# The front of a fused scan-and-experts kernel in another order, with list factors for eight columns at once

## The chip, the cores and the metric

The kernel runs on one core of one Trainium2 chip. The metric is the device time of one execution in microseconds (us), as the median of several runs. A profiled execution is shown beside it: its span runs from the first to the last recorded instruction, and its own time is a little longer than its span.

## The reference

For x of shape (2, 2048, 256) the layer norm xn (without weights) feeds two branches, and the result is x + scan branch + expert branch.

```python
x = L0_attn_x
xn = _layernorm(x, axis=-1)
x = x + _L0_attn_ref(xn, ...) + _L0_ffn_ref(xn, ...)

# scan branch: sort the tokens of each batch by nearest mean, scan, put them back
buckets = argmax(l2norm(xn) @ l2norm(means).T)          # 8 means
sort_idx = argsort(buckets, stable=True); xs = xn[sort_idx]
x_dbl = x_proj_weight @ xs                              # dts (32), B (16), C (16)
C += (means @ prompt_weight.T)[buckets of the sorted tokens]
delta = softplus(dt_projs_weight @ dts + bias); A = -exp(A_logs)
h = exp(delta*A)*h + delta*u*B; y = sum(h*C) + D*u      # 256 channels x 16 states
out = y in the old order of the tokens

# expert branch: 8 experts, the best two of each token
logits = xn @ w_gate; top 2; probs = softmax over the two
y_e = (silu(xn @ w1_e) * (xn @ w3_e)) @ w2_e            # hidden 512
out = sum over the two of probs * y_e
```

Both branches need an order of tokens that is known only at run time: the scan needs the tokens sorted by bucket, the experts need them in tiles of 128 that belong to one expert.

## The kernel before

**Front.** `normalize(b, xts)` is called once per batch (two batches of 2048 tokens, J = 16 columns of 128). It takes the statistics (L337 to L348), 1/sqrt by `rsqrt` (L244 to L253: a square root on ScalarE, L247, then a reciprocal and one Newton step on VectorE), normalises 16 columns in place (L358), writes them to the DRAM tensor `xn_d` (L362), transposes them (L370, L371) and multiplies with the normalised means and the gate weights (L374). After a second transpose, `sc` holds the bucket scores (L394) and `lg_all` the gate logits (L399).

`sort_tokens` (L404 to L456) finds each token's bucket and its position in the sorted order. `list_rows(b, pos)` (L458) turns positions into a list: which token stands at each position. `route` (L463) finds the two best experts, a slot for each of the 2 x 4096 choices, the expert of each of the NT = 71 tiles and hence the rows of the weights to load (`w_row`, L526), the list of tokens by slot (`token_of`, L510), and each token's share of the two experts, written beside the tokens into `xn_d` (L539).

`list_tokens` (L298 to L329) makes such a list with TensorE. For each column of 128 tokens a one-hot matrix of the place's low 7 bits (`one`, L315) is multiplied (L321) with a one-hot row of the high bits, scaled with two parts of the token's number (`num`, L317). The products of all columns add up in PSUM. The scan's list has 16 columns for one batch, the experts' list 64 columns. Both factors are built column by column on VectorE.

**Order of the front.** The text calls `normalize` for both batches, `sort_tokens`, `list_rows(0, pos)`, the gather of the first piece (L549), `route`, then the gathers of the first tiles' tokens (`load_rows`, L778) and weights (`load_up`, `load_down`, L764), then everything of the first scan piece up to its step sizes (`turn` L570, `project` L584, `end_projection` L589 to L592, `load_b` L609, `load_z` L597, `step_size` L621 to L627, `square` L631, `series` L642 to L651, `mask_z` L605). This part of the text is put on the engines by a scheduler that may move an instruction ahead of others on its own engine when it expects its inputs earlier. A pool of small tiles (`front`) is closed after `route`; the third set of weight buffers lies in the memory that it frees.

**The main stage** is in the order of the text on each engine (chained by the last lines of the kernel). Eight scan pieces (2 batches, 4 pieces of 512 tokens) give 64 steps of four places each; a place is one `feed` (L695), one `scan` (L704) on VectorE and one `decay` (L689) on ScalarE, with the turning (L716, L720) and contraction (L725) of the step before. Between the places the text deals out 213 expert jobs (71 tiles: two of `up`, L804, and one of `down`, L827), so that TensorE's and VectorE's planned work keep a fixed ratio. The first `ahead` = 5 jobs stand before the first scan place:

```python
ahead = 5
for n in range(ahead):
    jobs[n]()
    ...
pieces[0].begin(0)
pieces[0].begin(1)
for i in range(Q):
    steps[0].decay(i)
steps[0].feed(0)
```

`at_place(2, 3, lambda: list_rows(1, pos), 2.5, 7.0)` puts the second batch's list into the third step. When the last job is given, `acc_d` (which starts as a copy of x, L240, and takes the expert rows and the scan's rows) is copied to the output (L1026); the last piece is added there (L745).

Of the kernel before, what the change touches and what calls it, by code (L numbers as in the profile page):

```python
# [60 lines left out]
def scan_moe_kernel(  # L61
# [55 lines left out]
    slot = [cst.tile([P, BJ], I32, name=f"slot{k}") for k in range(2)]  # L117
# [14 lines left out]
    def load_x(b: int, j0: int, pool=tok):  # L132
# [18 lines left out]
    idx_l = cst.tile([P, BJ, K], F32, name="idx_l")  # L151
# [5 lines left out]
    idx_m = cst.tile([P, BK, J], F32, name="idx_m")  # L157
# [4 lines left out]
    keep = cst.tile([P, BK, J], F32, name="keep")  # L162
    nc.vector.memset(keep, 1.0)
    nc.vector.memset(keep[:, :, 0:1], 0.0)
    keep2 = cst.tile([P, E, BJ], F32, name="keep2")
# [8 lines left out]
    idx_p = cst.tile([P, 2, P], BF16, name="idx_p")  # L174
    nc.gpsimd.iota(
        idx_p, pattern=[[0, 2], [1, P]], base=0, channel_multiplier=0,
# [3 lines left out]
    token = cst.tile([P, BJ], I32, name="token")  # L180
    nc.gpsimd.iota(
        token.rearrange("p (b j) -> p b j", b=B), pattern=[[L, B], [1, J]], base=1,
        channel_multiplier=J,
    )
    parts = cst.tile([P, BJ, 2], F32, name="parts")
    for i, (op, by) in enumerate(((ALU.logical_shift_right, 6), (ALU.bitwise_and, 63))):
        part = cst.tile([P, BJ], I32, name=f"part{i}")
        nc.vector.tensor_scalar(part, token, by, None, op)
        nc.vector.tensor_copy(parts[:, :, i], part)
# [50 lines left out]
    nc.sync.dma_start(acc_d[0 : B * L, :], x.rearrange("b l d -> (b l) d"))  # L240
# [3 lines left out]
    def rsqrt(r, v, shape):  # L244

        s = sml.tile(shape, F32, tag="rs_s", name="rs_s")
        nc.scalar.activation(s, v, AF.Sqrt)  # L247
        nc.vector.reciprocal(r, s)
        t = sml.tile(shape, F32, tag="rs_t", name="rs_t")
        nc.vector.tensor_mul(t, v, r)  # L250
        nc.vector.tensor_mul(t, t, r)
        nc.vector.tensor_scalar(t, t, -0.5, 1.5, ALU.mult, ALU.add)
        nc.vector.tensor_mul(r, r, t)  # L253
# [29 lines left out]
    def over(v, last_dim):  # L283
        return v.unsqueeze(2).to_broadcast([P, v.shape[1], last_dim])

    def first_of_max(v, tag):

        n = v.shape[1]
        m = sml.tile([P, n], F32, tag=f"m{tag}", name="fm_m")
        nc.vector.tensor_reduce(m, v, AX.X, ALU.max)  # L290
        c = sml.tile([P, n, K], F32, tag="fm_c", name="fm_c")
        nc.vector.tensor_tensor(c, v, over(m, K), ALU.is_equal)
        nc.vector.tensor_mul(c, c, idx_l[:, 0:n, :])
        i = sml.tile([P, n], F32, tag=f"i{tag}", name="fm_i")
        nc.vector.tensor_reduce(i, c, AX.X, ALU.min)
        return m, i

    def list_tokens(places, parts, width: int, tag: str):  # L298


        pl = ps_m.tile([P, 2, width], F32, tag="m", name="pl")
        cols = []
        for k, place in enumerate(places):
            n = place.shape[1]
            fs = []
            for what, op, by in (("lo", ALU.bitwise_and, P - 1), ("hi", ALU.logical_shift_right, 7)):
                v = lst.tile([P, n], I32, tag=f"{tag}i", name="v", bufs=1)
                nc.vector.tensor_scalar(v, place, by, None, op)
                f = lst.tile([P, n], F32, tag=f"{tag}{what}{k}", name="f", bufs=1)
                nc.vector.tensor_copy(f, v)  # L310
                fs.append(f)
            cols += [(fs, i) for i in range(n)]
        for m, ((lo, hi), i) in enumerate(cols):
            one = lst.tile([P, P], BF16, tag="one", name="one")
            nc.vector.tensor_scalar(one, idx_p[:, 0, :], lo[:, i : i + 1], None, ALU.is_equal)  # L315
            num = lst.tile([P, 2, width], BF16, tag=f"num{tag}", name="num")
            nc.vector.scalar_tensor_tensor(  # L317
                num, idx_p[:, :, 0:width], hi[:, i : i + 1],
                parts[:, i, :].unsqueeze(2).to_broadcast([P, 2, width]), ALU.is_equal, ALU.mult,
            )  # L320
            nc.tensor.matmul(  # L321
                pl.rearrange("p a q -> p (a q)"), lhsT=one, rhs=num.rearrange("p a q -> p (a q)"),
                start=m == 0, stop=m == len(cols) - 1,
            )
        hi = lst.tile([P, width], F32, tag=f"{tag}h", name="hi", bufs=1)
        nc.vector.tensor_scalar_mul(hi, pl[:, 0, :], 64.0)
        tokens = lst.tile([P, width], F32, tag=f"{tag}t", name="tokens", bufs=1)
        nc.vector.tensor_add(tokens, hi, pl[:, 1, :])
        return tokens  # L329

    sc = cst.tile([P, BJ, K], F32, name="sc")

    def normalize(b: int, xts):
# [16 lines left out]
        rsqrt(rstd, ve, [P, J])  # L350


        psc = ps_h.tile([P, CH], F32, tag="h0", name="psc")
        for j0 in range(0, J, JC):
            xn = xts[j0 // JC]
            for i in range(JC):
                j = j0 + i
                nc.vector.tensor_scalar(  # L358
                    xn[:, i, 0:D], xn[:, i, 0:D], nm[:, j : j + 1], rstd[:, j : j + 1],
                    ALU.add, ALU.mult,  # L360
                )
# [42 lines left out]
    def sort_tokens():  # L404

        _, bk = first_of_max(sc, "b")
        oh = sml.tile([P, BK, J], F32, tag="oh1", name="oh")
# [50 lines left out]
    def list_rows(b: int, pos):  # L458
        own = slice(b * J, (b + 1) * J)
        tokens = list_tokens([pos[:, own]], parts[:, own, :], J, "s")  # L460
        nc.vector.tensor_scalar(line_of[b], tokens, -1.0, None, ALU.add)

    def route():  # L463
# [3 lines left out]
        m1, i1 = first_of_max(lg, "1")  # L467
        oh1 = sml.tile([P, BJ, E], F32, tag="oh1", name="oh1")
        nc.vector.tensor_tensor(oh1, idx_l, over(i1, E), ALU.is_equal)
        nc.vector.scalar_tensor_tensor(lg, oh1, LOWEST, lg, ALU.mult, ALU.add)  # L470
        m2, i2 = first_of_max(lg, "2")
        oh2 = sml.tile([P, BJ, E], F32, tag="oh2", name="oh2")
        nc.vector.tensor_tensor(oh2, idx_l, over(i2, E), ALU.is_equal)

        both = sml.tile([P, E, BJ], F32, tag="at", name="both")
        nc.vector.tensor_add(both.rearrange("p e j -> p j e"), oh1, oh2)
# [24 lines left out]
        for oh, s in ((oh1, slot[0]), (oh2, slot[1])):  # L501
            at = sml.tile([P, BJ, E], F32, tag="at", name="at_slot")
            nc.vector.tensor_mul(at, oh, cum.rearrange("p e j -> p j e"))
            sf = sml.tile([P, BJ], F32, tag="sf", name="sf")
            nc.vector.tensor_reduce(sf, at, AX.X, ALU.add)
            nc.vector.tensor_copy(s, sf)
        tokens = list_tokens(slot, parts, NT, "e")
        none = sml.tile([P, NT], F32, tag="none", name="none")
        nc.vector.tensor_scalar(none, tokens, 0.0, spare, ALU.is_equal, ALU.mult)
        nc.vector.scalar_tensor_tensor(token_of, tokens, -1.0, none, ALU.add, ALU.add)  # L510

# [26 lines left out]
        for b in range(B):  # L538
# [3 lines left out]
            )  # L542

# [293 lines left out]
    pos = sort_tokens()  # L837
    pieces = [Piece(b, c) for b in range(B) for c in range(NCH)]
    tiles = [Tile(t) for t in range(NT)]
    list_rows(0, pos)  # L840
    pieces[0].gather()
    route()
# [4 lines left out]
    for t in tiles[:NW]:  # L847
        t.load_rows()
        t.load_up()
    for t in tiles[:NW]:  # L850
        t.load_down()
# [68 lines left out]
    ahead = 5  # L920
# [159 lines left out]
```

## Time and profile before

| | us |
|---|---|
| median of 3 runs (lowest, highest) | 829.47 (824.61, 829.79) |
| the profiled execution's own time | 832.5 |
| its span | 830.7 |
| VectorE (DVE) busy | 740.2 |
| TensorE (PE) busy | 723.6 |
| GpSimd (POOL) busy | 526.3 |
| ScalarE (ACT) busy | 492.6 |

In the profile, PEld is TensorE's load of the stationary operand, SPq the queue that issues the plain DMAs, POOLq the one that issues the indirect ones, and L317 is line 317 of the kernel. Busy time is the time in which at least one instruction of the engine is recorded as running; one of TensorE's matmuls has a modelled end, so a busy TensorE is not one at its peak. A granted clock of 1.0 (PEclk) is the full TensorE clock. The duration of an instruction is longer than the distance between two starts where consecutive instructions overlap.

### The profile page before, as it was taken

How to read it: one execution, taken by the hardware profiler on the slowest of the kernel's cores; microseconds unless marked ns; L12 is line 12 of the kernel's file. 1: busy time of each engine (PE TensorE's matmuls, PEld its weight loads, DVE VectorE, ACT ScalarE, POOL GpSimd, SP SyncE). 2: the span in 40 equal slices, each digit the busy share in tenths (PEclk: the TensorE clock that was granted, in tenths of full speed). 3: DMA queues.
4: the chain of work that ended last, by engine and by line, in shares of the span. 5: the costliest groups of instructions: out<-in, count | busy, mean ns of one | idle time of the engine just before them, and what ended most of it. 6: DMA issues, size and time to landing. Idle time of an engine off the chain costs nothing.

```text
span 830.7 us, 17111 instructions
## 1 busy us (share of the span) xinstructions
PE 723.6 (87%) x6548; PEld 601.4 (72%) x6548; DVE 740.2 (89%) x1363; ACT 492.6 (59%) x957; POOL 526.3 (63%) x373
## 2 busy tenths in 40 slices
PE   0953759999999999999999998999899989999963
PEld 0322239678987889788878986799779977899842
DVE  7659888889988999999999995899889996999992
ACT  2420225476567767686668563866677666857662
POOL 1004047657777678788878886687767677677413
PEclk9975559999999999999999998999999999999996
DMA  9804732357446754684568366647754765334562
GB/s 298 295 37 47 289 99 61 79 144 250 120 116 165 230 142 114 157 255 122 134 159 257 75 185 145 177 103 206 209 130 102 245 188 112 93 59 125 97 203 39
DMA packets 61185, 125.92 MB, mean 152 GB/s; under 512 B 24488, under 2 KB 42064, under 8 KB 53808
## 3 DMA queue, kind: packets, MB, share of 16 engines
q0 software_dynamic: 40224, 65.03, 34.5%
q1 hardware_dynamic: 20880, 59.80, 20.8%
q8 instruction: 52, 0.85, 0.4%
q14 instruction: 29, 0.24, 0.1%
HBM read 180.06 MB, written 27.00 MB: 249 GB/s over the span
## 4 chain that ended last, share of the span: by engine, by line
PE 55%; DVE 8%; ACT 7%; DMA 6%; issue 4%; POOL 2%; POOLq 0%; SPq 0%; ACTq 0%; DVEq 0%
PE p_ps L804 23%; PE py L827 12%; PE pt_s L716 9%; PE y L725 5%; DMA xs<-xn,line_of 3%; DVE hs L704 3%; ACT ht L720 2%; DVE bu L695 2%; DMA out_dram<-acc 2%; PE px L584 1%; ACT da L689 1%; PE pt_g L787 1%; DMA acc<-yo,token_of 1%; PE pt_u L570 1%; PE px L589 1%
## 5 line engine op out<-in xcount | busy, mean ns | idle before, releaser
L804 PE MATMUL p_ps<-xT,w 128*128 128x128 f32 x2272 | 281.9, 280 | 0.8 <-ACT xT L789 0.5
L804 PEld LDWEIGHTS p_ps<-xT,w 128*128 128x128 f32 x2272 | 269.5, 195 | 15.5 <-issue 7.6
L704 DVE TENSOR_TENSOR_SCAN hs<-da,carry,bu 128x512 f32<-128x512 f32 x192 | 246.4, 1284 | 0.0
L689 ACT ACTIVATE da<-dl,na 128x512 f32<-128x512 f32 x256 | 183.1, 726 | 1.1 <-DVE hs L704 1.0
L745 POOL DMA_INDIRECT acc<-yo,token_of x71 | 143.4, 2020 | 54.9 <-ACT yo L831 18.3
L695 DVE TENSOR_TENSOR bu<-du,bt 128x512 f32<-128x512 f32 x256 | 173.9, 680 | 0.0
L720 ACT COPY ht<-pt_s 128x512 f32<-128x512 f32 x256 | 137.5, 593 | 22.8 <-PE pt_s L716 21.3
L716 PE MATMUL pt_s<-ident,hs 128*128 128x128 f32 x1024 | 136.9, 277 | 14.8 <-ACT ht L720 7.9
L827 PE MATMUL py<-w,g 128*128 128x256 f32 x568 | 135.6, 382 | 5.6 <-ACT u L571 2.3
L716 PEld LDWEIGHTS pt_s<-ident,hs 128*128 128x128 f32 x1024 | 116.4, 142 | 31.5 <-ACT ht L720 13.8
L778 POOL DMA_INDIRECT xg_sb<-xn,token_of x71 | 93.2, 1313 | 53.3 <-DVE token_of L510 32.0
L764 POOL DMA_INDIRECT w<-in_w_up_dram,w_row x71 | 91.1, 1284 | 52.7 <-PE p_ps L804 17.4
L827 PEld LDWEIGHTS py<-w,g 128*128 128x128 f32 x568 | 102.3, 190 | 19.4 <-ACT u L571 3.3
L764 POOL DMA_INDIRECT w<-in_w_down_dram,w_row x71 | 94.6, 1333 | 21.6 <-issue 14.0
L549 POOL DMA_INDIRECT xs<-xn,line_of x32 | 43.0, 1344 | 72.1 <-DVE fm_m L532 62.6
L812 ACT ACTIVATE t_sb<-p_ps 128x512 f32<-128x512 f32 x71 | 42.7, 601 | 65.1 <-PE p_ps L804 61.6
L704 DVE TENSOR_TENSOR_SCAN hs<-da,bu 128x512 f32<-128x512 f32 x64 | 78.3, 1223 | 1.1 <-ACT da L689 1.1
L831 ACT ACTIVATE yo<-py,own 128x256 f32<-128x256 f32 x71 | 34.1, 481 | 71.8 <-PE py L827 58.7
L725 PE MATMUL y<-ht,z 128*32 128x128 f32 x2048 | 75.2, 284 | 1.3 <-ACT ht L720 0.8
L817 DVE SCALAR_TENSOR_TENSOR t_sb<-t_sb,p_ps 128x512 f32<-128x512 f32 x71 | 48.3, 681 | 24.0 <-ACT t_sb L812 21.1
L725 PEld LDWEIGHTS y<-ht,z 128*32 128x32 f32 x2048 | 52.8, 112 | 23.0 <-issue 13.2
L745 POOL DMA_INDIRECT acc<-yt,line_of x28 | 50.9, 1818 | 21.6 <-issue 9.6
(198 smaller groups left out, 690.8 us busy)
## 6 DMA issues: line engine op xcount, KB each, us to landing
bt<-bc SPq DMA_DIRECT2D x32, 1024.0 KB
z<-bc SPq DMA_DIRECT2D x32, 256.0 KB
xn<-xt SPq DMA_DIRECT2D x8, 520.0 KB
xt<-in_x_dram SPq DMA_DIRECT2D x8, 512.0 KB
w<-in_w_up_dram,w_row POOLq DMA_INDIRECT x71
w<-in_w_down_dram,w_row POOLq DMA_INDIRECT x71
xg_sb<-xn,token_of POOLq DMA_INDIRECT x71
acc<-yo,token_of POOLq DMA_INDIRECT x71
```

What stands on the lines that cost most here:

```text
L689: nc.scalar.activation(self.da[i], self.piece.dl[:, self.h, :], AF.Exp, scale=na[:, self.h, n : n + 1])
L695: nc.vector.tensor_mul(self.bu[i], self.piece.du[:, self.h, :], self.piece.bts[self.q][:, i, :])
L704: nc.vector.tensor_tensor_scan(self.hs[:, :, i], self.da[i], self.bu[i], start, ALU.mult, ALU.add)
L716: nc.tensor.transpose(pt[:, j, :], self.hs[:, t0 : t0 + G, :].rearrange("p t n -> p (t n)"), ident)
L720: nc.scalar.copy(self.ht[i], pt)
L725: nc.tensor.matmul(p.ys[self.h][j * G : (j + 1) * G, i, :], lhsT=p.zs[q][:, i * (P // G) + j, :], rhs=self.ht[i][:, j, :], start=False, st ...
L745: ins = nc.gpsimd.indirect_dma_start(out=to, out_offset=bass.IndirectOffsetOnAxis(ap=numbers, axis=0), in_=rows, in_offset=None, compute_o ...
L764: nc.gpsimd.indirect_dma_start(out=to[self.t % NW], out_offset=None, in_=rows, in_offset=bass.IndirectOffsetOnAxis(ap=w_row[:, self.t : se ...
L778: nc.gpsimd.indirect_dma_start(out=self.xg, out_offset=None, in_=xn_d, in_offset=bass.IndirectOffsetOnAxis(ap=token_of[:, self.t : self.t ...
L804: nc.tensor.matmul(p[:, f, :], lhsT=wk[:, h, f * P : (f + 1) * P], rhs=self.xT[:, h, :], start=h == 0, stop=h == ND - 1,)
L817: nc.vector.scalar_tensor_tensor(self.s, self.s, 1.0, self.p1, ALU.add, ALU.mult)
L827: nc.tensor.matmul(py, lhsT=self.g[:, f, :], rhs=w2[:, f, :], start=f == 0, stop=f == NH - 1)
```

## The change

- **Order.** After `normalize` the text calls `route`, gathers the first three tiles' tokens and the first two tiles' weights, and only then calls `sort_tokens` and `list_rows(0, pos)` and gathers the first piece. The third set of weights is loaded after that, when the front's pool is closed. Inside `route` the list of the experts comes last, behind the weights' rows and the shares. Best-expert and bucket searches (`first_of_max`) run per batch. `ahead` is 14.
- **List factors.** `list_tokens` builds `one`, and the one-hot part of `num`, for LC = 8 columns in one VectorE instruction each, in bfloat16 with the column innermost; the two scaled parts of `num` are one ScalarE and one VectorE instruction for eight columns. The token's number is now 16 x partition + column instead of 64 x high part + low part. TensorE still makes one matmul per column, reading both factors with a step of eight elements.
- **1/sqrt.** `rsqrt` starts from an integer guess on the bits and makes three Newton steps, all on VectorE.
- **Smaller edits.** The last of each four columns is normalised on ScalarE; the copy of x into `acc_d` is issued after the writes of `xn_d`; some constants move to the front's pool.

```diff
-    idx_p = cst.tile([P, 2, P], BF16, name="idx_p")
+    LC = 8
+    idx_p = cst.tile([P, P, LC], BF16, name="idx_p")
...
-    nc.sync.dma_start(acc_d[0 : B * L, :], x.rearrange("b l d -> (b l) d"))
...
     def rsqrt(r, v, shape):
 
-        s = sml.tile(shape, F32, tag="rs_s", name="rs_s")
-        nc.scalar.activation(s, v, AF.Sqrt)
-        nc.vector.reciprocal(r, s)
+        guess = sml.tile(shape, I32, tag="rs_g", name="rs_g")
+        nc.vector.tensor_scalar(guess, v[:].bitcast(I32), 1, None, ALU.logical_shift_right)
+        nc.vector.tensor_scalar(
+            r[:].bitcast(I32), guess, -1.0, float(0x5F3759DF), ALU.mult, ALU.add
+        )
         t = sml.tile(shape, F32, tag="rs_t", name="rs_t")
-        nc.vector.tensor_mul(t, v, r)
-        nc.vector.tensor_mul(t, t, r)
-        nc.vector.tensor_scalar(t, t, -0.5, 1.5, ALU.mult, ALU.add)
-        nc.vector.tensor_mul(r, r, t)
+        for _ in range(3):
+            nc.vector.scalar_tensor_tensor(t, v, -0.5, r, ALU.mult, ALU.mult)
+            nc.vector.tensor_mul(t, t, r)
+            nc.vector.scalar_tensor_tensor(r, t, 1.5, r, ALU.add, ALU.mult)
...
-        for m, ((lo, hi), i) in enumerate(cols):
-            one = lst.tile([P, P], BF16, tag="one", name="one")
-            nc.vector.tensor_scalar(one, idx_p[:, 0, :], lo[:, i : i + 1], None, ALU.is_equal)
-            num = lst.tile([P, 2, width], BF16, tag=f"num{tag}", name="num")
-            nc.vector.scalar_tensor_tensor(
-                num, idx_p[:, :, 0:width], hi[:, i : i + 1],
-                parts[:, i, :].unsqueeze(2).to_broadcast([P, 2, width]), ALU.is_equal, ALU.mult,
-            )
-            nc.tensor.matmul(
-                pl.rearrange("p a q -> p (a q)"), lhsT=one, rhs=num.rearrange("p a q -> p (a q)"),
-                start=m == 0, stop=m == len(cols) - 1,
-            )
+        for m in range(n // LC):
+            own = slice(m * LC, (m + 1) * LC)
+            one, num = factors(width)
+            nc.vector.tensor_tensor(
+                one, idx_p, lo[:, own].unsqueeze(1).to_broadcast([P, P, LC]), ALU.is_equal
+            )
+            nc.vector.tensor_tensor(
+                num[:, 2], idx_p[:, 0:width, :], hi[:, own].unsqueeze(1).to_broadcast([P, width, LC]),
+                ALU.is_equal,
+            )
+            b = of_batch[m]
+            j0 = m * LC % J
+            nc.scalar.activation(num[:, 0], num[:, 2], AF.Copy, scale=part_p[:, b : b + 1])
+            nc.vector.tensor_mul(
+                num[:, 1], num[:, 2],
+                part_j[:, j0 : j0 + LC].unsqueeze(1).to_broadcast([P, width, LC]),
+            )
+            for i in range(LC):
+                nc.tensor.matmul(
+                    pl, lhsT=one[:, :, i], rhs=num[:, 0:2, :, i],
+                    start=m == 0 and i == 0, stop=m == n // LC - 1 and i == LC - 1,
+                )
...
     for b in range(B):
         normalize(b, xts[b * NCH : (b + 1) * NCH])
-    pos = sort_tokens()
+    nc.sync.dma_start(acc_d[0 : B * L, :], x.rearrange("b l d -> (b l) d"))
     pieces = [Piece(b, c) for b in range(B) for c in range(NCH)]
     tiles = [Tile(t) for t in range(NT)]
+    route()
+    for t in tiles[:NW]:
+        t.load_rows()
+    for t in tiles[: NW - 1]:
+        t.load_up()
+        t.load_down()
+    pos = sort_tokens()
     list_rows(0, pos)
     pieces[0].gather()
-    route()
     front.close()
     late = ctx.enter_context(tc.tile_pool(name="late", bufs=1))
     w13_sb.append(late.tile([P, 2 * ND * H], F32, name=f"w13_{NW - 1}"))
     w2_sb.append(late.tile([P, NH * D], F32, name=f"w2_{NW - 1}"))
-    for t in tiles[:NW]:
-        t.load_rows()
-        t.load_up()
-    for t in tiles[:NW]:
-        t.load_down()
+    tiles[NW - 1].load_up()
+    tiles[NW - 1].load_down()
...
-    ahead = 5
+    ahead = 14
```

The new factor tiles of the front lie in the buffers that held x (`front_factors`); those of `list_rows(1, pos)` in the main stage in two tiles of their own (`late_factors`).

## The prediction

> **What bounds the kernel now.** I read the page's busy tenths first (40 slices of 20.8 us; a 9 is 90% or more).
>
> ```profile
> PE   0953759999999999999999998999899989999963
> DVE  7659888889988999999999995899889996999992
> PEclk9975559999999999999999998999999999999996
> ```
>
> From slice 7 on both engines are full, so the main stage is bounded by TensorE and VectorE together. Slices 3 to 6 (50 to 118 us) are a front in which VectorE is full, TensorE nearly idle and its clock at half. The table by stretches (columns: stretch, length, then busy us of PE, PEld, DVE, ACT, POOL; clock; DMA share; GB/s) puts figures to it.
>
> ```profile
> 21.20:50.70 29.50, 27.42 (x104) 10.79 (x104) 14.94 (x61) 12.46 (x23) 0.00 (x0) 1.00 0.62 227
> 50.70:77.90 27.20, 5.33 (x31) 3.72 (x30) 25.21 (x117) 0.83 (x2) 6.16 (x6) 0.54 0.13 22
> 77.90:118.40 40.50, 25.53 (x86) 9.46 (x87) 36.90 (x146) 11.13 (x18) 7.00 (x7) 0.54 0.57 165
> 160.00:790.00 630.00, 604.21 (x5734) 526.38 (x5734) 586.32 (x864) 421.28 (x829) 467.08 (x308) 0.99 0.57 152
> ```
>
> Normalising (21 to 51) is TensorE's (27.4 of 29.5 us). The next 67.7 us are VectorE's (62.1). In the main stage TensorE has 604 of 630 us, VectorE 586. Who gives way there is told by the waits of that stretch: VectorE's longest are for products of TensorE.
>
> ```profile
> DVE t_sb L817 <- ACT t_sb L812: 17.5, 13, 3.2
> DVE g L821 <- PE p_ps L804: 13.1, 9, 5.6
> ```
>
> So a place lasts as long as TensorE needs. The timeline names what the front hands over, and when.
>
> ```profile
> 16.31 1.28 ACT L247 ACT_TABLE_LOAD   x1
> 17.61 0.20 ACT L247 ACTIVATE rs_s<-msq 8x1 f32<-8x1 f32 x1
> 66.53 0.17 DVE L461 TENSOR_SCALAR line_of<-tokens 128x16 int32<-128x16 f32 x1
> 112.61 0.23 DVE L510 SCALAR_TENSOR_TENSOR token_of<-tokens,none 128x71 int32<-128x71 f32 x1
> 113.11 1.18 POOL L778 DMA_INDIRECT xg_sb<-xn,token_of  x1 [31.98 <-DVE token_of L510]
> 118.59 8.46 PE L804 MATMUL p_ps<-xT,w 128*128 128x128 f32 x64
> 127.72 1.29 DVE L695 TENSOR_TENSOR bu<-du,bt 128x512 f32<-128x512 f32 x2
> ```
>
> The scan's list is ready at 66.7, but its first `bu` starts at 127.7: the piece's series waited on VectorE behind the experts' list (109.6), and the five jobs put before the scan start only at 118.6, because the tokens' gather waited for `token_of` at 112.8. The groups of that list:
>
> ```profile
> L317 DVE SCALAR_TENSOR_TENSOR num<-idx_p,f,parts 128x142 bf16<-128x142 bf16 x64 | 22.9, 358 | 0.0
> L315 DVE TENSOR_SCALAR one<-idx_p,f 128x128 bf16<-128x128 bf16 x80 | 19.8, 248 | 3.6 <-PE pl L321 3.6
> L321 PE MATMUL pl<-num,one 128*128 128x142 bf16 x64 | 15.8, 279 | 13.4 <-DVE num L317 13.2 <-issue 0.2
> L514 DVE TENSOR_TENSOR ge<-idx_t,end 128x568 f32<-128x568 f32 x1 | 0.7, 746 | 0.0
> ```
>
> **The change, part by part**, on the profiled run's clock.
>
> *1/sqrt and the columns on ScalarE.* Before, the table load at 16.31 and the root at 17.61 hold the first normalised column until 20.8. Now eleven small VectorE operations, some 0.21 apart like L250 to L253, give `rstd` near 17. But the first product (L374, 23.4 before) also needs the means, whose row lands at 15.8: the last bn_stats end at 17.1, then eleven operations, product, transpose and copy: 20.6. I take 3 us, between 1 (VectorE is 77% busy before 21.2 and gets some 12 more operations there) and 5. After it TensorE's 16 rounds of 1.56 us set the pace as before. Here a rule and the trace differ: the Trainium skill, page "ScalarE: Activation LUTs", section "What ACT_TABLE_LOAD costs", puts about 2.66 us on every switch of tables. Four switches less would be 10.6 us. The rows are 1.28 us each, and only the first lies on the path (the one at 50.0 hides behind L382, the one at 28.0 behind TensorE's rounds). I follow the rows. ScalarE's eight columns (some 0.6 us each) fit: it has 12.5 of 29.5 us there. Last logits: 50.7 - 3 = 47.7.
>
> *Route first.* The logits' copy ends 0.5 later. Twelve operations on half the tokens (0.29 each from L394; a dependent one starts about 0.32 after the last) are 3.8; the first batch's share runs under the transposes. From L478 to L506 before, scan, TensorE's counts, base and slots take 7.5 us with fillers, and 6 without: slots at 58. Tile experts and shares (L514 to L526, L530 to L537, together 3.0) now stand ahead of the list, and the halves of the slots cost 0.8: 61.8.
>
> *The list.* 64 times 0.44 us (0.16 + 0.28, starts of L315 and L317) and 3.6 of waits for TensorE become eight groups. No bfloat16 operation with two tensors is in the trace. The nearest is L514, the same compare at fp32: 746 ns for 568 elements, and with L293's 417 ns for 256 that is 147 ns + 1.05 ns an element, less 0.09 of overlap. At that rate a group (1024 + 568 + 568) is 1.14 + 0.66 + 0.66 = 2.46 us. A rule speaks against the edit: the Trainium skill's page "VectorE: DVE Perf Modes", section "The perf-mode tier table (the rule you actually need)", caps two-tensor operations at 2x in bfloat16, where the tensor_scalar that goes may have 4x. By it a group is 0.60 + 0.36 + 0.36 = 1.3, 1.4 with the product waiting for its input: half the rate, but one fixed cost for eight. I take 2x[...]: 8 x 1.4 = 11.2; the other end is 19.7. ScalarE's part (0.75 from L689's 726 ns for 512) is shorter than a group. TensorE needs 8 x 0.12 a group (four L321 at 93.0 took 0.65 at half clock; less one's 0.28, over three). The last group's products and four operations: 2.2. `token_of`: 61.8 + 11.2 + 2.2 = 75.2, against 112.8.
>
> *Tokens, weights, first jobs.* From `token_of` to the first product took 118.6 - 112.8 = 5.8: now 81. The weights' rows are known at about 62, so four loads (1.3 us of POOL each, 3 MB at 252 to 290 GB/s, 11 us) land by 80. If the scheduler leaves them behind the tokens' gathers, that costs 8. The shares' write moves from 74.5 (it had waited for the piece's gathers) to 62 and lands long before. The copy into `acc_d` now stands behind the eight `xn` writes, ahead of the shares: 4.2 MB at 301 GB/s, over by 55; the first add is past 90. Uncovered it would cost 14.
>
> *Edits at nothing.* The new constants cost GpSimd under 2 us (L158 made 256 elements in 0.41), which idles from 4.4 to 67; `idx_p` is read first near 62, and without that cover its microsecond would stand before the list. Four operations on token parts (L188, L189, 0.25 each) leave VectorE's full start, within the 1 to 5 above.
>
> *Sort and scan list behind it.* What is left of the sort on VectorE is some 7 us, then `list_rows(0)` with two groups 3 to 4, and small TensorE steps that queue behind jobs: `line_of` at 88, against 66.7. The first piece is gathered 11 us later (66.7 to 78.0 before), turned and projected (10.5 before, at half clock and between list products): its `xd` is at 108. Then `bt` lands some 8 later, and series and masks are 16 x 0.61 = 9.8 from 111. So piece 0 is ready at 121.
>
> *Fourteen jobs.* Five run from 81 to 92. The sixth adds a wait: for the third weights, whose buffers are free only after the scan's list, issued behind the piece's gathers (94) and landed at 100. Behind it on TensorE queue the other eight jobs and the scan's steps, and VectorE's first `bu` stands behind those jobs' gates. Nine jobs (six of 1.79, three of 1.73, three turns: 16.6) and piece 0's 7 us of TensorE end at 123. First `bu` at 122.5: 5.2 earlier.
>
> *Main stage.* TensorE has 16.6 less to do after that, and no longer trickles through 16 list products (158.1 to 162.4): 19.4. VectorE loses three tiles (4.7) and 3 of the 7.0 of `list_rows(1)`. From 127.7 to 814.6 it was busy 641.7 of 686.9, 93.4%. I take 17 off: then 94.6%, less than the 99% of the stretch from 720 to 790, so it can follow. The tail (last add, output copy) moves along.
>
> **Sum:** 5.2 + 17 = 22 off. The profiled 832.5 becomes 810.5; the median shown is 3.0 under its profiled run, so 829.5 - 22 = 807.5.
>
> **Rivals.**
>
> *Two-tensor operations at the fp32 rate.* Plus 8.5 in the list, 1 in the scan's: everything after moves by 9 to 10. 817. For it: no row shows the mode. Against: L315's spacing.
>
> *The text's order on TensorE.* If piece 0's `pt_u`, `px` and `pd` stand ahead of the jobs in TensorE's order, jobs start at 109, cold (the first ones at half clock, 4 us), 14 take 27 + 4, and `bu` comes at 141: 22 - 18.5 = 3.5 off, 826. Against: before, the scheduler mixed L570 with L321 by readiness.
>
> *Slower: TensorE chokes on factors read with a step of eight.* Both operands of 64 products are now strided; no row of the trace has that. At 0.12 each they hide under VectorE. From about 0.18 each they set the list's pace; all the gain is gone when the 64 take 11 + 22 = 33 us, 0.52 each. At 0.75 (load and product six times as long, unhidden) the list takes 48: plus 37, 844. Against: the Trainium skill's page "TensorE: Matmul & The Clock Gate", section "Weight-path perf modes — Fast Weight Load (FWL) and DoubleRow", allows the fast load any column step up to 1,024; nothing here shows it.
>
> *More.* The front's waits overlap better: piece 0 ready at 112, jobs through by then: 33 off, 796.
>
> **How the numbers follow.** Forecast 0.53 (its own range 798 to 815), fp32 rate 0.17, text's order 0.09, strided operands 0.10, more 0.11. The range 790 to 831 holds all but the strided case and the ends. 1% (8.3 us: 821 to 838) is about what a measurement of this kernel can tell from no change. Faster by over 1%: forecast, fp32 rate, most of more: 0.79. Within: text's order and pieces of the others 0.10. Slower 0.11.
>
> **What would show it.** Right: `token_of` near 75; the compare of 1024 elements near 0.69 us (1.22 is the rival); the first L804 near 81; 14 jobs before the first `bu` near 122; main-stage DVE near 95%. Wrong: list products over 0.2 us apart; TensorE idle from 92 past 105 for the third weights; a first `bu` past 135; or VectorE at its limit with the same length of the main stage, which would mean that the nine jobs were not what held it.

## The result: 3.5% slower

| | before | after |
|---|---|---|
| median of the runs compared (us) | 827.04 (four runs, 823.6 to 829.79) | 855.64 (four runs, 854.99 to 856.17) |
| the profiled execution's own time, span (us) | 832.5, 830.7 | 855.74, 854.0 |
| granted TensorE clock over the span | 0.941 | 0.922 |

The ratio is 1.035 (95% interval 1.030 to 1.040). The forecast was 807.5 with a range of 790 to 831. In all that follows a time is the median of all executions, a ratio is taken over the faster ones alone (so it is not always the quotient of two medians), and the trace of experiment 3 is of a slower execution (852.48 us), read only for which waits and half-clock stretches there are.

The busy tenths of the page after, in slices of 21.4 us:

```profile
PE   0847379998998999999998997999799979899963
DVE  7667353977997899999998997899789997899992
PEclk9975569998998999999998998999899999999996
```

The place to look is slices 4 to 6, counted from 0 (85 to 149 us), where the forecast had TensorE full of jobs: TensorE is a 3 in slice 4 and VectorE 3, 5, 3, where before VectorE had 8, 8, 8. So the list did get cheaper on VectorE, but nothing took the time that it left. In the rest of the span the clock has five 8s; before had one.

The timeline after, with the hand-overs of the front (start, duration, engine, line, operation; in brackets the idle time before it and its releaser):

```profile
65.75 0.19 DVE L545 CAST slot<-sf 128x64 int32<-128x64 f32 x1
88.44 0.22 DVE L583 SCALAR_TENSOR_TENSOR token_of<-tokens,none 128x71 int32<-128x71 f32 x1
95.49 0.17 DVE L490 TENSOR_SCALAR line_of<-tokens 128x16 int32<-128x16 f32 x1
102.02 1.51 PE L611 MATMUL pt_u<-ident,xs 128*128 128x128 f32 x6 [6.99 <-DMA xs<-xn,line_of]
114.79 0.69 PE L828 MATMUL pt_g<-ident,xg_sb 128*128 128x128 f32 x2
119.43 2.93 PE L845 MATMUL p_ps<-xT,w 128*128 128x128 f32 x12
147.87 1.30 DVE L736 TENSOR_TENSOR bu<-du,bt 128x512 f32<-128x512 f32 x2
```

The slots are ready at 65.9 (forecast 58), `token_of` at 88.7 instead of 112.8 (75.2). Yet the first product of an expert starts at 119.4, later than before (118.6), and the first `bu` comes at 147.9 instead of 127.7. TensorE had waited 7 us for piece 0's rows (L611), and only when `pt_u`, `px` and `pd` were through did the first `pt_g` run, at 114.8, although the tokens of tile 0 were read by VectorE at 91.7. From the first scan place to the last, before took 683.2 us (130.15 to 813.33) and after 686.3, in spite of nine jobs less (first line before, second after):

```profile
130.15:813.33 683.18, 648.69 (x6184) 562.64 (x6186) 639.14 (x949) 456.78 (x895) 495.65 (x326) 0.98 0.57 151
150.33:836.63 686.30, 640.54 (x6058) 553.85 (x6060) 629.91 (x911) 455.17 (x888) 477.47 (x315) 0.96 0.55 149
```

VectorE is busy for 629.9 us of the 686.3 (91.8%; the forecast said 94.6%), and the mean clock is 0.96 where before had 0.98. So of the 45 us between the forecast's 810.5 and the profiled 855.7, 25 arose before the first `bu` and 20 after it (17 expected to go, 3 added).

### The profile page after: what moved, and what is told of

It is laid out like the page before. It is cut to its first block, busy times and chain, and to the rows that moved or that the text cites. A ratio compares the mean times of both kernels' runs of the same rounds, so it can differ in the third digit from the quotient of the medians.

```text
span 854.0 us, 17020 instructions
## 1 busy us (share of the span) xinstructions
PE 736.0 (86%) x6548; PEld 613.0 (72%) x6548; DVE 716.4 (84%) x1237; ACT 499.6 (58%) x968; POOL 522.1 (61%) x374
## 3 DMA queue, kind: packets, MB, share of 16 engines
q1 hardware_dynamic: 20880, 59.80, 20.2%
## 4 chain that ended last, share of the span: by engine, by line
PE 62%; DMA 10%; ACT 9%; DVE 7%; POOL 6%; issue 5%; POOLq 0%; SPq 0%; ACTq 0%; DVEq 0%
PE p_ps L845 24%; PE py L868 12%; PE pt_s L757 9%; PE y L766 5%; DMA xs<-xn,line_of 3%; DMA acc<-yo,token_of 2%; PE pl L325 2%; POOL acc L786 2%; PE psc L397 2%; PE px L625 2%; DMA out_dram<-acc 2%; ACT ht L761 2%; POOL xs L590 2%; ACT da L730 2%; ACT sq L672 1%
## 5 line engine op out<-in xcount | busy, mean ns | idle before, releaser
L845 PEld LDWEIGHTS p_ps<-xT,w 128*128 128x128 f32 x2272 | 271.4, 196 | 11.3 <-issue 6.2
L786 POOL DMA_INDIRECT acc<-yo,token_of x71 | 138.8, 1955 | 76.5 <-ACT yo L872 41.6
L805 POOL DMA_INDIRECT w<-in_w_up_dram,w_row x71 | 86.4, 1217 | 128.0 <-DVE slot L545 60.1
L868 PE MATMUL py<-w,g 128*128 128x256 f32 x568 | 144.3, 400 | 14.0 <-ACT r L666 10.4
L757 PEld LDWEIGHTS pt_s<-ident,hs 128*128 128x128 f32 x1024 | 118.8, 144 | 30.3 <-ACT ht L761 12.4
L868 PEld LDWEIGHTS py<-w,g 128*128 128x128 f32 x568 | 107.7, 200 | 30.2 <-ACT r L666 11.6
L805 POOL DMA_INDIRECT w<-in_w_down_dram,w_row x71 | 97.2, 1369 | 21.6 <-issue 16.5
L862 DVE SCALAR_TENSOR_TENSOR g<-t_sb,p_ps 128x512 f32<-128x512 f32 x71 | 48.2, 679 | 12.5 <-PE p_ps L845 10.8
```

Of the source, the lines that this page charges most:

```text
L757: nc.tensor.transpose(pt[:, j, :], self.hs[:, t0 : t0 + G, :].rearrange("p t n -> p (t n)"), ident)
L786: ins = nc.gpsimd.indirect_dma_start(out=to, out_offset=bass.IndirectOffsetOnAxis(ap=numbers, axis=0), in_=rows, in_offset=None, compute_o ...
L805: nc.gpsimd.indirect_dma_start(out=to[self.t % NW], out_offset=None, in_=rows, in_offset=bass.IndirectOffsetOnAxis(ap=w_row[:, self.t : se ...
L845: nc.tensor.matmul(p[:, f, :], lhsT=wk[:, h, f * P : (f + 1) * P], rhs=self.xT[:, h, :], start=h == 0, stop=h == ND - 1,)
L868: nc.tensor.matmul(py, lhsT=self.g[:, f, :], rhs=w2[:, f, :], start=f == 0, stop=f == NH - 1)
```

## The experiments

Two questions: what the nine extra jobs cost, ahead of the scan and behind it; and what each part of the change (list, root, order) is worth by itself. A ratio is to the kernel before on the same chip (828.5 to 829.0 there).

**1. The changed kernel with 5 jobs ahead.**

```diff
-    ahead = 14
+    ahead = 5
```

> The changed kernel with 5 jobs instead of 14 ahead of the first scan place. Theory: the main stage lasts as long as VectorE and its waits make it, so the nine extra jobs ahead only delay the first bu: it comes near 130 us (piece 0 is ready on VectorE at 127.4, five jobs from 119.4 end near 130), the main stage keeps its 703 to 706, and the time is 838 (834 to 842). Rival, the forecast's: TensorE sets the places, so nine jobs more after the first bu cost 17 us there, and the time stays at 855 (851 to 859).

Measured: 829.12, ratio 1.000 (0.997 to 1.003). First `bu` at 129.1, main stage (first scan place to last) 675.0. The whole loss of the change is in this one number; all the other edits together come out even.

```profile
129.13 1.29 DVE L736 TENSOR_TENSOR bu<-du,bt 128x512 f32<-128x512 f32 x2
131.59:806.59 675.00, 645.25 (x6188) 560.99 (x6186) 635.88 (x923) 458.14 (x898) 497.21 (x326) 0.99 0.56 153
```

The rival falls: the main stage is not longer with nine jobs more, but 11.3 us shorter. The theory was right on the front and too weak on the main stage, where it expected no difference. TensorE's busy time says that something odd goes on: the nine jobs are 16.6 us by the forecast's count, but TensorE is busy only 4.7 us less without them (640.5 against 645.3). Its idle time in the stage, length less busy time, went from 29.8 to 45.8.

**2. The kernel before with 14 jobs ahead.**

```diff
-    ahead = 5
+    ahead = 14
```

> The kernel before with 14 jobs instead of 5 ahead of the first scan place, nothing else. Theory (VectorE and its waits set the main stage): first bu near 127.7 + 17 = 145, main stage unchanged, time 844 (840 to 848). Rival (TensorE sets the places): what is put ahead is taken off behind, time 827 (823 to 831).

Measured: 856.4, ratio 1.031 (1.026 to 1.035): more than the theory said. First `bu` at 148.05 (20.3 later), main stage 691.5 (8.3 longer). The old kernel with the changed constant alone is as slow as the changed kernel.

```profile
148.05 1.29 DVE L695 TENSOR_TENSOR bu<-du,bt 128x512 f32<-128x512 f32 x2
150.51:842.01 691.50, 644.08 (x6062) 556.01 (x6060) 633.58 (x937) 455.18 (x887) 485.18 (x315) 0.96 0.54 148
```

**Where the main stage's extra time is.** I read the granted clock of each of these traces in windows of 1 us between 150 and 790. TensorE runs at half clock in stretches of 4 to 8 us:

| | jobs ahead | stretches | us in them | main stage, us |
|---|---|---|---|---|
| before | 5 | 4 | 23 | 683.2 |
| after | 14 | 8 | 56 | 686.3 |
| after with 5 (1.) | 5 | 3 | 13 | 675.0 |
| before with 14 (2.) | 14 | 9 | 60 | 691.5 |

Those of before, after and experiment 1 each have a gap of TensorE of 1.4 to 3.1 us just before them, or one into which they begin; the exception is the first of before, at 162, which follows the sixteen products of the second batch's list with pauses of some 0.15 us between them. One of the changed kernel, by windows (columns as in the table by stretches: PE, PEld, DVE, ACT, POOL, clock, DMA share, GB/s) and by its instructions:

```profile
724.00:727.00 3.00, 3.00 (x40) 1.52 (x38) 2.97 (x7) 2.63 (x5) 2.39 (x3) 1.00 1.04 337
727.00:731.00 4.00, 0.87 (x5) 0.23 (x3) 4.00 (x6) 4.00 (x9) 0.52 (x1) 1.00 0.27 70
731.00:735.00 4.00, 4.00 (x13) 3.25 (x14) 2.61 (x4) 1.24 (x4) 0.00 (x0) 0.57 0.01 4
735.00:738.00 3.00, 3.00 (x29) 3.00 (x28) 0.82 (x2) 2.78 (x6) 2.49 (x2) 1.00 0.23 20
```

```profile
727.40 0.44 PE L828 MATMUL pt_g<-ident,xg_sb 128*128 128x128 f32 x2
729.66 0.67 ACT L665 ACTIVATE e<-pd,bias 128x512 f32<-128x512 f32 x1
730.23 0.68 ACT L666 ACTIVATE r<-pd,bias 128x512 f32<-128x512 f32 x1
730.97 3.45 PE L868 MATMUL py<-w,g 128*128 128x256 f32 x8 [3.13 <-ACT r L666]
```

A `down` job stands here right behind the step size of the next piece. Its `py` needs a PSUM buffer that still holds `pd`, and ScalarE has two squares, two decays and more to do before it reads `pd` (L665, L666: `e` and `r`). TensorE idles for 3.1 us, and then does its next work at half clock (0.57 in the 4 us after): eight products of `py` take 3.45 us, where undisturbed ones take 1.89:

```profile
409.62 1.89 PE L868 MATMUL py<-w,g 128*128 128x256 f32 x8
```

The waits of the main stage show that this is a pattern (us in total, times, longest):

```profile
PE pt_u L611 <- DMA xs<-xn,line_of: 18.1, 12, 2.5
PE py L868 <- ACT r L666: 10.4, 5, 3.1
DVE t_sb L858 <- ACT t_sb L853: 25.9, 11, 5.1
```

```profile
PE pt_u L611 <- DMA xs<-xn,line_of: 9.4, 6, 2.2
PE py L868 <- ACT r L666: 1.1, 2, 0.6
DVE t_sb L858 <- ACT t_sb L853: 17.5, 13, 4.0
```

The first three lines are the changed kernel's, the other three those of experiment 1. With 14 ahead a job meets the same place of every piece: the plan's arithmetic puts one behind the second step size (place 16) in all of the first seven pieces, a `down` in three of them, the first, fourth and seventh. The changed kernel's three waits of `py` of 3.0 to 3.1 us are in just these pieces (up to 200.3, 459.7 and 731.0), and a stretch at half clock goes with each. With 5 ahead the jobs drift against the pieces: five have a job at place 16, none of them a `down`. Of the other five stretches of the changed kernel four go with waits for the rows of the next piece (`pt_u`) and one with a wait for `num` of the second batch's list.

The 11.3 us between the changed kernel and experiment 1 are then made up like this: TensorE idles 16.0 us more, and is busy 4.7 less, not the 16.6 (an estimate) that nine jobs are worth; the missing 11.9 would be work done at half clock. The clock leaves room for it: over the windows the sum of 1 - clock is 23.9 us in the changed kernel and 5.1 in experiment 1. How much of the loss is the gaps and how much the clock behind them, no run separates.

**3. 14 jobs ahead, dealt half a job later.**

```diff
-    pe_now = dve_now = 0.0
+    pe_now, dve_now = 1.0, 0.0
```

> The changed kernel, still 14 jobs ahead; the planner's count of TensorE work starts at 1.0 instead of 0, so every later job stands about half a job later. By the plan's own arithmetic no job is then dealt right behind the step size of the next piece (place 16 of a piece), where with 14 jobs one falls in every piece. Theory: the main stage with 14 is 11 us longer than with 5 because of where its jobs stand: TensorE waits there for the step size's ScalarE work and for the piece's gather, 2 to 3 us, and each such gap is followed by half clock. Then the waits of py for ACT r (10.4 us in 5) go, the clock comes back to 0.98, the main stage takes 676 to 680 instead of 686, time 847 (843 to 850). Rival (with nine jobs fewer TensorE has gaps wherever the jobs stand): 855 (853 to 858).

Measured: 843.52, ratio 1.018 (1.012 to 1.025), at the lower end of what the theory expected and 12 us under the changed kernel's 855.6. The waits in its trace:

```profile
PE py L868 <- ACT r L666: 0.7, 3, 0.3
PE pt_u L611 <- DMA xs<-xn,line_of: 14.2, 7, 3.1
```

The waits of `py` are gone, four half-clock stretches (23 us) are left of eight. The rival (fewer jobs mean gaps wherever they stand) falls. What remains over experiment 1 is 14.4 us, less than the 18.7 to 20.2 by which 14 jobs delay the first scan place (150.33 in the changed kernel, 151.78 here, against 131.59): well placed, nine jobs less are worth some 4 to 6 us to the main stage (with the interval of this run, 6 more or less), not 17. The shift moves every job, so that it shows the place to be the cause, and not which of the places.

**4. The list factors alone, on the kernel before.** `list_tokens` and its helpers are those of the change; order, roots and 5 jobs are as before.

```diff
-        for m, ((lo, hi), i) in enumerate(cols):
-            nc.vector.tensor_scalar(one, idx_p[:, 0, :], lo[:, i : i + 1], None, ALU.is_equal)
...
+        for m in range(n // LC):
+            nc.vector.tensor_tensor(
+                one, idx_p, lo[:, own].unsqueeze(1).to_broadcast([P, P, LC]), ALU.is_equal
+            )
...
```

> The kernel before with the new list factors alone (eight columns at once in bfloat16, read with a step of eight by TensorE); order, roots and the 5 jobs as before. Theory: 64 products at about 0.26 us set the list's pace, 17 to 18 us instead of 34, so token_of comes near 97 (112.8 before), the first product of an expert near 103, piece 0's series may now be what is late; first bu near 115, time 815 (810 to 820). Rival (reading with a step of eight is so slow that nothing is won): token_of near 110, time within 4 us of 827.

Measured: 823.35, ratio 0.990 (0.987 to 0.992). `token_of` at 102.2, first product of an expert at 111.2, first `bu` at 125.9, main stage 675.9. The time is in the rival's band (823 to 831), the list is not: `token_of` gains 10.7 us where the rival had 3. But the first `bu` gains only 1.8: the list products fill TensorE, and piece 0's `pd` stands behind the last of them (101.0; before, the first at 88.5), so that the series begins at 108.4, hardly earlier than before (109.6). The other 7.3 us are in the main stage: 3.5 of them in the first piece, where the second batch's list lies (89.5 instead of 93.0), the rest in later pieces, whose work is as it was.

**5. The root alone, on the kernel before.**

```diff
-        nc.scalar.activation(s, v, AF.Sqrt)
-        nc.vector.reciprocal(r, s)
...
+        nc.vector.tensor_scalar(guess, v[:].bitcast(I32), 1, None, ALU.logical_shift_right)
...
+        for _ in range(3):
...
```

> The kernel before with 1/sqrt on VectorE alone. Forecast's step: the first normalised column comes 3 us earlier and with it all that follows, so 824. What the changed kernel's trace suggests: VectorE is full before 21 us, the eleven small operations take the place of the table load and cost as much or more, the last logits come at 50.7 to 53 instead of 50.7: 827 to 830. A difference of 3 us either way is what this run can tell.

Measured: 833.49, ratio 1.005 (1.002 to 1.008). The last scores of batch 1, first in the kernel before, then here:

```profile
50.75 0.29 DVE L394 TENSOR_TENSOR sc<-pb,rn 128x128 f32<-128x128 f32 x1 [5.98 <-PE pb L382]
54.71 0.29 DVE L396 TENSOR_TENSOR sc<-pb,rn 128x128 f32<-128x128 f32 x1 [7.18 <-PE pb L384]
```

The root on VectorE costs 4 us up to here; the forecast took 3 off. The timeline shows where they begin: the last bn_stats end at 18.2 instead of 17.1, and the eleven operations for `rstd` run mixed with the same eleven for the means, so `rstd` is ready at 23.2 instead of 20.7. I read this as VectorE being the engine that lacks time there, and not ScalarE with its table load of 1.28 us; what adds the rest between 23.2 and the scores was not followed. Of the 4 us the first `bu` shows 1.9 (129.6).

**6. `num` with the column outermost** (on experiment 1), so that TensorE reads its moving operand without a step; `one` keeps its step of eight.

```diff
-  num = tok.tile([P, 3, width, LC], BF16, ...)
+  num = tok.tile([P, 3, LC, width], BF16, ...)
...
-  pl, lhsT=one[:, :, i], rhs=num[:, 0:2, :, i],
+  pl, lhsT=one[:, :, i], rhs=num[:, 0:2, i, :],
```

> The changed kernel with 5 jobs ahead, and num with the column outermost, so that TensorE reads its moving operand without a step; one, the stationary operand, is still read with a step of eight. Theory: the moving operand is what made a product 0.26 us (with 32 columns in the scan's list it is 0.08, with the same stationary operand), so a product falls to about 0.12, VectorE sets the list's pace again, 11 to 15 us, token_of near 82 to 85 instead of 88; line_of 90 to 92, first bu 125, time 825. Rival (the stationary operand's load is what is slow): products stay at 0.25 us and token_of at 88. What the broadcast on the inner axis does to VectorE's 0.45 us for 568 elements is read too: 0.45 or 0.66.

Measured: 825.85, ratio 0.994 (0.991 to 0.996); `token_of` at 84.7, first `bu` at 125.6. The groups of the front (busy us, mean ns of one; idle before it), first the changed kernel, then this experiment:

```profile
L325 PE MATMUL pl<-num,one 128*128 128x142 bf16 x64 | 16.9, 437 | 8.9 <-DVE num L320 8.9
L310 DVE TENSOR_TENSOR one<-idx_p,f 128x1024 bf16<-128x1024 bf16 x10 | 6.8, 685 | 2.3 <-PE pl L325 2.3
L313 DVE TENSOR_TENSOR num<-idx_p,f 128x568 bf16<-128x568 bf16 x8 | 3.6, 456 | 0.0
```

```profile
L331 PE MATMUL pl<-num,one 128*128 128x142 bf16 x64 | 9.3, 325 | 13.6 <-DVE num L326 13.2 <-ACT num L325 0.3
L319 DVE TENSOR_TENSOR num<-idx_n,f 128x568 bf16<-128x568 bf16 x8 | 6.0, 751 | 0.0
```

And the first eight products of each, in the timeline:

```profile
69.37 2.25 PE L325 MATMUL pl<-num,one 128*128 128x142 bf16 x8 [8.94 <-DVE num L320]
```

```profile
68.91 1.17 PE L331 MATMUL pl<-num,one 128*128 128x142 bf16 x8 [9.57 <-DVE num L326]
```

Eight products take 2.25 us with the step in `num` and 1.17 without, both at half clock and both with `one` read by eights: 0.26 against 0.12 from start to start, (2.25 - 0.44) / 7 and (1.17 - 0.33) / 7 with the groups' means for the last one. The 0.12 is what products took before the change, when neither operand had a step. So the stationary operand's step costs nothing in the distance between products (its recorded loads, 163 ns in the mean against 109 before, are longer but overlap), which agrees with the rule that the forecast had weighed (the Trainium skill, page "TensorE: Matmul & The Clock Gate", section "Weight-path perf modes — Fast Weight Load (FWL) and DoubleRow": fast load with any column step up to 1,024); the moving operand's step of 16 bytes halves its rate. On VectorE the other layout costs its price: a broadcast on the inner axis is 751 ns for 568 elements instead of 456. A group is then 1.92 us (starts of L316 at 71.36 and 73.28), between the forecast's 1.4 and its rival's 2.46, and still faster than the 2.1 that TensorE needs for a group in the changed kernel.

**7. The five jobs first** (on experiment 1): the block of piece 0 is moved behind them.

```diff
-    p = pieces[0]
-    for h in range(ND):
-        p.turn(h)
...
     for n in range(ahead):
         jobs[n]()
...
+    p = pieces[0]
+    for h in range(ND):
+        p.turn(h)
...
```

> The changed kernel with 5 jobs ahead, and these five with their turns placed in the text before piece 0's turning, projection and step size. Theory: the jobs started at 117 to 119 only because piece 0's products stand ahead of them on TensorE; now the first p_ps comes at 93 to 96, the five end by 106, in TensorE's wait for the piece's gather (7 us) and a little after; piece 0 is 2 to 3 later, first bu 122 to 125 instead of 129, time 823 (820 to 827). Rival (something else than the order holds the jobs: weights or tokens not there): first p_ps past 105, time 829 or more.

```profile
93.84 1.49 PE L845 MATMUL p_ps<-xT,w 128*128 128x128 f32 x6
125.24 1.29 DVE L736 TENSOR_TENSOR bu<-du,bt 128x512 f32<-128x512 f32 x2
```

The first product of an expert starts at 93.8 instead of 117.3: tokens and weights had been there. First `bu` at 125.2, 3.9 earlier. The time, 826.3, is too uncertain (four runs, 813.8 to 827.2) to tell from experiment 1 or from before; the place of the wait is shown by the trace, its price only roughly. What is late next is the step size: VectorE waits 8.5 us for the first square, to 113.9.

**8. Experiment 4 with 2 jobs ahead.**

```diff
-    ahead = 5
+    ahead = 2
```

> The kernel before with the new list factors, and 2 jobs ahead instead of 5. Theory: five jobs from 111 to 125 are what holds the first bu there (series begin at 108, piece 0 is ready near 119), so it comes near 120, the main stage keeps its 676, time 818 (814 to 822). Rival: three jobs more in the main stage or their other places give it back, 823 to 828.

Measured: 828.79, ratio 0.998 (0.996 to 1.001). First `bu` at 121.0 as expected, but the main stage is 690.4, 14.5 longer: three jobs more and other places give everything back, and which of the two does it is not shown. The rival was right. What the number of jobs ahead is worth cannot be read from the front alone, in either direction.

**9 and 10. Two versions without the losses.** One keeps the changed order (route first) with the jobs first, `num` by rows and the old root; the other keeps the order before, with the new list factors and `num` by rows. Both have 5 jobs ahead. The edits are those shown under 4, 5 (undone), 6 and 7.

> The changed order with three of its losses taken out together: 5 jobs ahead, placed in the text before piece 0's products; num with the column outermost; and the old 1/sqrt (square root on ScalarE, reciprocal and one Newton step). Theory: the single gains add up: line_of from 95 to 91.6 by the list, 2 less by the root, jobs in the wait for the gather; first p_ps near 88, first bu 119 to 121, main stage 676 to 680, time 819 (816 to 823). Rival (the losses overlap, the z rows that piece 0 writes and reads back come last): first bu not before 123, time 824 or more.

> The order before, old roots, 5 jobs, with the new list factors and num with the column outermost. Theory: the list is VectorE's 1.92 us a group, token_of near 98 to 99 (101.9 with the step in num), and TensorE, no longer full of list products, gets to piece 0's px and pd earlier; first p_ps 106 to 108, first bu 120 to 122, time 818 (815 to 821). Rival (in this order the list runs beside piece 0's products, and what is late is ScalarE's and the gather's part): bu 125, time 823 as with the step.

Measured: 814.95, ratio 0.982 (0.979 to 0.985), for the changed order; 810.21, ratio 0.976 (0.972 to 0.981), for the order before. Both beat both kernels, and by more than their theories expected (819 and 818); the second is 45 us under the changed kernel's 855.6. Its front:

```profile
93.64 0.69 DVE L670 SCALAR_TENSOR_TENSOR dl<-sq,e 128x512 f32<-128x512 f32 x1 [2.44 <-ACT sq L659]
96.64 0.23 DVE L538 SCALAR_TENSOR_TENSOR token_of<-tokens,none 128x71 int32<-128x71 f32 x1
102.83 3.39 PE L832 MATMUL p_ps<-xT,w 128*128 128x128 f32 x18
112.00 1.28 DVE L723 TENSOR_TENSOR bu<-du,bt 128x512 f32<-128x512 f32 x2
```

Piece 0's `pd` now runs between the list's products (87.1), so its series begins at 93.6, in VectorE's wait for the tokens, and only the five jobs stand before the first `bu` at 112.0 (120 to 122 expected). With the changed order it comes at 120.1: there piece 0 has no list left to hide behind, and its rows, projection and step size come last (first series at 108.8). So with the other losses gone the order costs 8 us in the front (the two medians differ by 4.7); the forecast let piece 0 be ready at 121 and counted on jobs to fill the time until then.

## Why the prediction was wrong

- **"A place lasts as long as TensorE needs", 17 us off the main stage: wrong, and the largest single error (20 us).** I took TensorE's 604 of 630 us and VectorE's waits for TensorE as proof that TensorE set the pace. The longer of the two waits shown, 17.5 us, is one for ScalarE, which waits for the product in its turn; and a wait for a product can come from the place of a job as well as from the amount of work. Experiments 1 to 3 show that nine jobs less are worth some 4 to 6 us there when they stand well, and that where they stood the stage grew by 11. In the third piece of the changed kernel, one without a half-clock stretch, both engines are at their end, VectorE a little more than TensorE (80.54 and 79.47 of 81.17 us):

```profile
336.25:417.42 81.17, 79.47 (x776) 69.55 (x778) 80.54 (x117) 58.31 (x117) 66.65 (x42) 1.00 0.61 165
```

  Elsewhere a half clock makes TensorE's busy time longer for the same work. In the kernel before that is at most 8.5 of the 604 us (the sum of 1 - clock over its windows), so I take the main fault to be that the forecast reckoned with one engine where two are nearly full and the order decides which of them waits. The forecast's own last sign of error came true in its weaker form: the same length of the main stage, with VectorE at 92%.
- **The jobs start at 81 and run in TensorE's idle time: wrong by the order.** The rival "the text's order on TensorE" (0.09) is what happened: it gave 109 for the start, 141 for the first `bu` and 826, and had the main stage's 17 us in it, which did not come. The argument against it, that the scheduler had mixed `pt_u` with list products, did not carry over: when it put the order out, it left the jobs behind the whole of piece 0. Experiment 7 shows for five jobs that the order alone held them. The forecast's own plan, fourteen jobs ahead of piece 0's products, was not run.
- **The third weights** were no limit: their loads were issued at 95.9 and 102.2, and the jobs came later.
- **The list at 0.12 us a product: mis-sized on TensorE, right on VectorE.** VectorE's 1.33 us a group (starts of L310 at 68.27 and 69.59) is the forecast's 1.3 to 1.4, at twice the fp32 rate; L315's spacing, 0.16 us for 128 elements where the forecast's fp32 fit gives 0.19, had been no more than a hint, since that operation reads one tensor only. TensorE needed 0.26 a product, above the 0.18 at which the rival "strided operands" let it take the pace, and half of the 0.52 at which all was lost: from the first group (67.0) to `token_of` (88.7) it took 21.7 us instead of 13.4. The rival did not say which operand; experiment 6 shows that it is the moving one.
- **3 us off the rounds by the root: wrong sign.** It is 4 us on by experiment 5; with ScalarE's columns the changed kernel's last scores come at 53.0 instead of 50.75. Against the forecast's 47.7 that moves all that follows by 5.3.
- **Route and slots:** 13.0 us from the last scores to the slots against 10.3 forecast; the list's start, on the other hand, came 1.1 us after the slots and not 3.8, because the scheduler put shares and tile experts beside it.
- **Weights and copy into `acc_d`:** no cost, as forecast. The weights' loads were issued from 66.1, long before their use. The copy cost nothing for another reason than the forecast's: its issue did not move behind the writes of `xn_d`, the scheduler issued it at 16.75 (before at 15.92).

The parts, taken one by one: list -5.5, root +4.7, five jobs instead of 14 giving 829.1, so that what is left for the order is 829.1 - 828.8 + 5.5 - 4.7 = 1 us, less than these runs can tell from zero. It holds the smaller edits too, none of which was run alone. The nine jobs are +26.5 (855.64 - 829.12).

## What to carry to other kernels

An engine at 96% busy is not yet the bound: look at a stretch without stalls and see which engine's work is as long as that stretch, then test it by moving a piece of its work out. Work put ahead of a pipeline delays all of it; it pays only in time that is idle and only if it stands in the engine's order where the idle time is, which must be read from the order and not hoped from a scheduler. When interleaved work changes by a few items, look where the items land relative to the periodic work: a constant that shifts them by half an item was worth some 12 us here.

## What was not expected of the hardware

- Gaps of TensorE of 1.4 us (a wait for `num`, up to 180.67) to 3.1 us were often followed within about 2 us by 3.5 to 7 us at half clock; the wait of 3.1 us shown above cost its own length and 1.6 us more in the next eight products. It is not a fixed rule. Two waits of the kernel before, for the same thing:

```profile
243.34 0.33 PE L570 MATMUL pt_u<-ident,xs 128*128 128x128 f32 x1 [1.98 <-DMA xs<-xn,line_of]
593.57 0.33 PE L570 MATMUL pt_u<-ident,xs 128*128 128x128 f32 x1 [2.25 <-DMA xs<-xn,line_of]
244.00:247.00 3.00, 3.00 (x36) 2.61 (x27) 2.86 (x6) 1.49 (x4) 1.72 (x2) 0.50 0.44 44
594.00:597.00 3.00, 2.54 (x42) 2.03 (x35) 3.00 (x5) 2.61 (x6) 1.51 (x1) 1.00 0.62 182
```

  The first was followed by half clock, the second, longer one was not. Over all twelve traces, between 150 and 790 us, by their clock records, half clock began in the gap or within 2.5 us of its end in 17 of 41 gaps of 1.3 to 2 us, in 27 of 33 of 2 to 3 us, and in all 11 of 3 us or more (gaps that begin at half clock not counted). The Trainium skill, page "TensorE: Matmul & The Clock Gate", section "HAM oscillation — how this bites in real kernels", warns of idle gaps over some 3.4 us; here, by these counts, shorter ones were often enough.
- A moving operand in bfloat16 read with a step of eight elements runs at half the rate (0.26 against 0.12 us for 142 columns at half clock); the same step in the stationary operand did not show.
- VectorE compares two bfloat16 tensors at about twice the fp32 rate also when one is broadcast over a middle axis (456 ns for 568 elements, 746 at fp32), and loses that when the broadcast is on the inner axis (751 ns).
